# A conv and mixture-of-experts kernel: token tiles in a pool of their own, and the last group's gamma multiply inside the threshold search

## The chip, the cores and the metric

The kernel runs on one core of a Trainium2 chip. The time is that of one execution on the device, in microseconds. Before the change three runs took 4796.59, 4796.63 and 4800.55 us; the median, 4796.63 us, is what a prediction is compared with. One more execution was recorded by the hardware profiler, and every row shown below comes from that one. The engines are called PE (matrix products), DVE (vector), ACT (activation functions), POOL (GpSimd) and SP, which here issues DMAs.

## What is computed

Two layers follow each other. The first is a depthwise 7x7 convolution, a layer norm over channels and a mixture of eight experts with a capacity for each expert; the second is a dilated convolution with an attention in the frequency domain. The change touches only the first, cut here to what matters:

```python
x = depthwise_conv7x7(input) + dw_bias          # 32 x 128 x 56 x 56
xf = layernorm(x) * ln_gamma + ln_beta          # 100352 tokens of 128
topv, topi = top_k(xf @ Wg + bg, 2)             # two of 8 experts
wts = softmax(topv); priority = wts[:, 0]
order = argsort(-priority)                      # tokens by priority
cap = int(1.25 * T / 8)                         # 15680 places an expert
keep = position_in_expert(topi[order]) < cap
y = W2[e] @ gelu(W1[e] @ xf[token] + b1[e]) + b2[e]     # kept pairs
out = input + xf + layer_scale * sum(gate * y)
```

A token keeps its place with an expert if it is among the `cap` tokens of highest priority for that expert. The kernel doesn't sort. For each expert it looks for the threshold of priority by a search over counts, and makes a list of the tokens above it.

## The kernel before

**Conv stage (lines 121 to 391).** Eight groups of images are worked through. A group's tokens are the tile `y` (L376), 98 tokens in each of 128 partitions, 128 channels each, which is 50,176 bytes a partition; there are two such tiles, in the pool `a2`. `conv` fills `y`. Then `block` (L186) does seven pieces of a group (six of 16 tokens, one of 2) in phases: `stats`, `across` (transposes), `norm` (scale and shift by ACT, and by POOL too in the last group), `logits`, `back` and `affine` (L227). `affine` multiplies the normed tokens by gamma (tile `gB`) on DVE at L231 and stores them to the DRAM tensor `xf` at L235. `choose` (L307) takes logits to the two chosen experts (`first1`, `first2`) and their weights (`w1`, `w2`). The phases of a group run beside the conv of the next one. The last group (`end`) has no such neighbour: `plan` (L357) puts its `norm` and `affine` last, `affine` takes up to 8 tokens at a time, at a lower priority, and its stores go out on SP's queue.

**From the last choice to the first list (L507 to L1136).** Pools are laid out as stacks from two sides of the memory. When the conv stage's pools (`a1`, `a2`, `a4`, `a5`) have closed, `b1` and `b2` are opened on the left, and `c1` to `c4`, for the experts, on the right. A pool that is laid where an older one was waits for all of that one's users. After that come, in the order of the source:

- the loads of constants `below`, `lane`, `iota` (into `b1`), of the experts' weights W1 and W2, of `b1t`, `b2t`, `bC` and `lsB` (into `c1`), all on SP's queue, L517 to L529; a small tile `zrow` in `c1`, cleared by DVE at L552;
- `search0` (L677), the search for expert 0. `priorities` (L585) writes `key`; then 12 rounds follow, each with two counts by ACT (`sign`, L702) and one by DVE (`junk`, L706), a sum across partitions by PE (`pn`, L713) and two small DVE steps (`met`, L714, and `lo`, L717). Beside the rounds it does one step each of a list `beside`: eight copies (L671) of transposed choices, made by `turns` (L659), and the keys of expert 0 in their final layout. It ends with `room` (L731);
- `ready` (L558), set-up of tiles for the list, at a lower priority;
- `shift` (L540): 32 products on PE of W1 with the layer norm's beta, L545, added to the experts' bias at L549;
- `listing` (L750) for expert 0: masks, ranks, starts, ten bit steps that move the tokens into place, and the list `ids` (L942). It needs `room` and tiles of `b2`. `search0`, `shift` and `listing` take turns in one single bank of PSUM (`rbank`, L400);
- `fetch` (L1013): gathers of tokens from `xf` by POOL and the experts' matmuls (L1048, L1066).

The order of an engine's instructions is made when the program is built: from the source's order and priorities, and from what the framework takes to be able to run. On the chip each engine takes its queue as it stands.

Of the kernel before, what the change touches and what calls it, by code (L numbers as in the profile page):

```python
# [30 lines left out]
F32 = mybir.dt.float32  # L31
# [7 lines left out]
C = 128  # L39
# [6 lines left out]
E = 8  # L46
# [28 lines left out]
def conv_seq_kernel(ctx: ExitStack, tc: tile.TileContext, t: dict, out: bass.AP, dbg: dict):  # L75
# [43 lines left out]
    w1, w2 = [rk.tile([128, FW], F32, name=f"w{r}") for r in (1, 2)]  # L119

    TG = 2 * NP
    with tc.tile_pool(name="a1", bufs=1) as a1, tc.tile_pool(name="a2", bufs=2) as a2, tc.tile_pool(
# [5 lines left out]
        gB = load(a1, "gB", [128, C], rowbc(t["ln_gamma"], 128))  # L128
# [57 lines left out]
        def block(g, y, lg, t0, n, end):  # L186
# [39 lines left out]

            def affine():  # L227
                with tc.high_priority(offset=-1000) if end else nullcontext():
                    for a in range(0, n, 8 if end else n):
                        cut = slice(a, min(n, a + 8) if end else n)  # L230
                        nc.vector.tensor_tensor(  # L231
                            out=yb[:, cut], in0=yb[:, cut],
                            in1=gB.unsqueeze(1).broadcast_to([128, cut.stop - a, C]), op=ALU.mult,
                        )
                    (nc.sync if end else nc.scalar).dma_start(  # L235
                        out=xfv[:, g * TG + t0 : g * TG + t0 + n, :], in_=yb
                    )
# [137 lines left out]
        for g in range(HI // 2):  # L375
            y = a2.tile([128, TG, C], F32, name="y")  # L376
            for k in range(NS):
                conv(g, k * CB, y)
                if (g, k) == (0, 2):
                    centre()  # L380
                for phase in behind.pop(k, []):
                    phase()
            for k in sorted(behind):
                for phase in behind[k]:
                    phase()
            behind = plan(g, y)
# [122 lines left out]
    b1 = lists_.enter_context(tc.tile_pool(name="b1", bufs=1))  # L509
    b2 = lists_.enter_context(tc.tile_pool(name="b2", bufs=2))  # L510
    experts = ExitStack()
    c1 = experts.enter_context(tc.tile_pool(name="c1", bufs=1, side="right"))
    c2 = experts.enter_context(tc.tile_pool(name="c2", bufs=2, side="right"))
    c3 = experts.enter_context(tc.tile_pool(name="c3", bufs=3, side="right"))
    c4 = experts.enter_context(tc.tile_pool(name="c4", bufs=4, side="right"))
    if True:
        below = load(b1, "below", [128, 128], t["below"])  # L517
# [52 lines left out]
        key = b1.tile([128, E, FW], F32, name="key")  # L570
        share = {}

        apart = set()

        def due(w, f):

            share[f] = w
            return f

        def later(f):  # L580

            apart.add(f)
            return f

        def priorities(e, to=None, cut=slice(0, R), n=FW):  # L585
            to = key[:R, e, :] if to is None else to
            other = b2.tile([128, FW], F32, name="junk", tag="junk")[cut, :n]
            for out_, f in zip((to, other), firsts):
                nc.vector.scalar_tensor_tensor(
                    out=out_, in0=f[cut, :n], scalar=float(E - e), in1=w1[cut, :n], op0=ALU.is_equal, op1=ALU.mult  # L590
                )
            nc.vector.tensor_tensor(out=to, in0=to, in1=other, op=ALU.add)

        thr = b1.tile([128, E], F32, name="thr")
        room = b1.tile([128, E], F32, name="room")

        def search(e0, n):
# [8 lines left out]
            def count(op, at, e):  # L606
                junk = b2.tile([128, FW], F32, name="junk", tag="junk")
                nc.vector.tensor_scalar(
                    out=junk[:R],
                    in0=key[:R, e, :],  # L610
                    scalar1=at[:R],
                    scalar2=None,
                    op0=op,
                    op1=ALU.add,
                    accum_out=part[:, e - e0 : e - e0 + 1],
                )
# [41 lines left out]

        def turns():  # L659

            todo = []
            for a in (w1, *firsts, w2):
                for m0 in range(0, NB, 4):
                    nm = min(4, NB - m0)
                    pt = bank("pkt")
                    for m in range(nm):
                        nc.tensor.transpose(
                            pt[:R, m * 128 : (m + 1) * 128], a[:, bass.DynSlice(m0 + m, R, step=NB)], ident
                        )
                    todo.append(  # L670
                        lambda a=a, pt=pt, m0=m0, nm=nm: nc.vector.tensor_copy(  # L671
                            a[:R, m0 * 128 : (m0 + nm) * 128], pt[:R, : nm * 128]
                        )
                    )
            return todo

        def search0():  # L677


            first = key[:, E - 1, :J]  # L680
            priorities(0, first, slice(0, 128), J)
            k0 = key[:, E - 2, :J]
            beside = turns() + [lambda: priorities(0)]
            lo = b1.tile([128, 1], F32, name="lo")
            nc.vector.tensor_scalar(
                out=k0, in0=first, scalar1=-0.5, scalar2=2.0**24, op0=ALU.add, op1=ALU.mult
            )
            nc.vector.memset(lo, 0.0)
            part = b1.tile([128, 3], F32, name="part0")
            trial = b1.tile([128, 1], F32, name="trial0")  # L690
            less = b1.tile([128, 2], F32, name="less0")
            met = b1.tile([128, 3], F32, name="met0")
            num = b1.tile([128, 1], F32, name="num0")
            for k in range(22, -1, -2):
                q = float(1 << k)
                nc.vector.tensor_scalar(
                    out=less, in0=offs[:, k // 2, :], scalar1=lo, scalar2=None, op0=ALU.subtract
                )
                nc.vector.tensor_scalar(out=trial, in0=lo, scalar1=q, scalar2=None, op0=ALU.add)
                for i in range(2):  # L700
                    sign = b1.tile([128, J], I16, name="sign", tag="sign")
                    nc.scalar.activation(  # L702
                        sign, k0, AF.Sign, bias=less[:, i : i + 1], accum_out=part[:, 1 + i : 2 + i]
                    )
                junk = b2.tile([128, FW], F32, name="junk", tag="junk")
                nc.vector.tensor_scalar(  # L706
                    out=junk[:, :J], in0=k0, scalar1=trial, scalar2=None, op0=ALU.is_ge, op1=ALU.add,
                    accum_out=part[:, 0:1],
                )
                if beside:  # L710
                    beside.pop(0)()
                pn = rbank("pn")
                nc.tensor.matmul(pn[:, :3], lhsT=ones, rhs=part, start=True, stop=True)  # L713
                nc.vector.scalar_tensor_tensor(  # L714
                    out=met, in0=pn[:, :3], scalar=1.0, in1=caps, op0=ALU.mult, op1=ALU.is_ge, accum_out=num
                )
                nc.vector.scalar_tensor_tensor(  # L717
                    out=lo, in0=num, scalar=q, in1=lo, op0=ALU.mult, op1=ALU.add
                )
            nc.vector.tensor_scalar(  # L720
                out=thr[:, 0:1], in0=lo, scalar1=2.0**-24, scalar2=0.5, op0=ALU.mult, op1=ALU.add
            )
            assert not beside
            junk = b2.tile([128, FW], F32, name="junk", tag="junk")
            nc.vector.tensor_scalar(
                out=junk[:, :J], in0=first, scalar1=thr[:, 0:1], scalar2=None, op0=ALU.is_gt, op1=ALU.add,
                accum_out=trial,
            )
            pn = rbank("pn")
            nc.tensor.matmul(pn[:, :1], lhsT=ones, rhs=trial, start=True, stop=True)  # L730
            nc.vector.tensor_scalar(  # L731
                out=room[:, 0:1], in0=pn[:, :1], scalar1=-1.0, scalar2=float(cap + 1), op0=ALU.mult, op1=ALU.add
            )


        caps = b1.tile([128, 3], F32, name="caps")
        nc.gpsimd.memset(caps[:, 0:1], float(cap))
        nc.gpsimd.memset(caps[:, 1:3], float(2 * cap - 128 * J))
        offs = b1.tile([128, 12, 2], F32, name="offs")
        for k in range(12):  # L740
            for i in range(2):
                nc.gpsimd.memset(offs[:, k, i : i + 1], 0.5 - (2 + i) * 4.0**k)
# [7 lines left out]
        def listing(e, ids, gates):  # L750
# [204 lines left out]
            def slots(r, s):  # L955
# [5 lines left out]
                mine = b2.tile([128, FW], F32, name="junk", tag="junk")[:R]  # L961
# [164 lines left out]
        search0()  # L1126
# [548 lines left out]
```

## Time and profile before

| what | us |
|---|---|
| median of three runs | 4796.63 |
| profiled execution (its span) | 5234.6 (5232.8) |
| PE busy in the span | 4638.2 (89%) |
| DVE busy in the span | 2815.0 (54%) |
| one store of 1 MB after another, rate | 283 to 284 GB/s |
| DVE L231 in the last group: first start, last start | 719.6, 740.2 |
| stores `xf<-y` on SP: first, second, last issue | 727.0, 733.8, 747.3 |
| first ACT count of the search | 761.85 |
| PE L545 (`shift`), begin and length | 809.56, 13.8 |
| list `ids` made (DVE L942) | 871.8 |

The profiled execution is 9% longer than the median run; so a stretch of it is compared with other stretches of it, and only then with the runs. The stores before the search, issue by issue: one of 128 KB at 727.0, then six of 1 MB at 733.8, 735.3, 736.8, 739.9, 743.6 and 747.3. How to read a row of the timeline: start, duration, engine, line, operation, the tile written and those read, their shapes, the number of instructions, and in brackets the idle time before it with what ended that. A row of the waits: who waited, on whom, us in total, how often, the longest. Durations of neighbouring DVE rows overlap by about 0.08 us, so the step from one start to the next is shorter than the duration.

### The profile page before, as it was taken

Reading aid. Unit: us, or ns where it says so; the run is one execution under the profiler, and the core shown is the slowest. Engines: PE = TensorE matmul, PEld = TensorE weight load, DVE = VectorE, ACT = ScalarE, POOL = GpSimd, SP = SyncE. Lnnn points to the kernel's source line nnn. Section 1 sums busy time; section 2 is a strip of 40 time slices with the busy share of each in tenths; the row PEclk is TensorE's granted clock in tenths of the full one; section 3 lists DMA queues with packets and bytes.
Section 4 is the critical chain, followed back from the end, with each engine's and each line's share of the span. In section 5 each row is a group of like instructions: output and inputs, shape, how many; then the busy total and the mean of one; then the engine's idle time right before and its main releaser. Section 6 shows DMA issues by size and latency. Waiting matters only on the chain.

```text
span 5232.8 us, 87253 instructions
## 1 busy us (share of the span) xinstructions
PE 4638.2 (89%) x33034; PEld 3216.6 (61%) x33034; DVE 2815.0 (54%) x5851; ACT 2079.8 (40%) x4260; POOL 2610.5 (50%) x2633
## 2 busy tenths in 40 slices
PE   8888844999999999999988799999998888888889
PEld 7777733777777767777766455555555555455556
DVE  4787876868685846442212245555444444444456
ACT  3576742444444444444433133333332222232234
POOL 0000022555555666666466566666566666666650
PEclk9999966999999999999999899999999999999999
DMA  9988940222222323333465455555565565545552
GB/s 254 275 254 261 260 128 17 65 61 66 70 69 71 83 79 87 84 87 87 126 173 135 119 153 161 156 146 151 145 163 150 150 159 155 151 128 151 155 147 57
DMA packets 767736, 705.23 MB, mean 135 GB/s; under 512 B 73231, under 2 KB 679568, under 8 KB 763220
## 3 DMA queue, kind: packets, MB, share of 16 engines
q1 hardware_dynamic: 597060, 487.55, 31.5%
q0 software_dynamic: 81664, 167.15, 14.6%
q10 hardware_dynamic: 88592, 44.96, 3.0%
q8 instruction: 261, 4.28, 0.4%
q14 instruction: 159, 1.30, 0.1%
HBM read 472.99 MB, written 226.39 MB: 134 GB/s over the span
## 4 chain that ended last, share of the span: by engine, by line
PE 74%; DVE 11%; issue 4%; another core or an unknown queue 4%; DMA 3%; ACT 3%; POOL 0%; SPq 0%; DVEq 0%; ACTq 0%; POOLq 0%
PE py L1066 17%; PE ph L1048 16%; PE pf L1283 15%; PE pm L1334 8%; PE pt L1326 4%; DVE st L196 2%; PE pxt L1031 2%; DVE y L231 2%; PE pg L1358 2%; PE pre L1423 2%; DMA xf<-y 2%; ACT y L222 2%; PE pim L1424 2%; PE pxs L1268 2%
## 5 line engine op out<-in xcount | busy, mean ns | idle before, releaser
L444 POOL DMA_INDIRECT y<-yf,slot x1568 | 1547.0, 987 | 972.2 <-issue 352.9
L1025 POOL DMA_INDIRECT xg<-xf,ids x861 | 908.8, 1055 | 710.5 <-PE py L1066 226.8
L1066 PEld LDWEIGHTS py<-W,hT 128*128 128x128 f32 x7872 | 927.2, 192 | 138.9 <-issue 117.1
L1066 PE MATMUL py<-W,hT 128*128 128x128 f32 x7872 | 947.6, 277 | 33.5 <-issue 33.4
L1283 PE MATMUL pf<-xp,cw 128*64 128x448 f32 x4032 | 927.0, 570 | 7.3 <-issue 6.0
L1048 PE MATMUL ph<-xT,W 128*128 128x512 f32 (+1 forms) x1984 | 905.5, 596 | 0.2 <-issue 0.2
L1051 ACT ACTIVATE hT<-ph,b1t 128x512 f32<-128x512 f32 (+1 forms) x992 | 616.7, 672 | 188.2 <-PE ph L1048 129.9
L1313 DVE COPY mid<-pt 112x512 f32<-112x512 f32 (+3 forms) x480 | 310.2, 661 | 572.4 <-PE pt L1326 220.3
L1100 ACT ACTIVATE yo<-yo,gates 128x128 f32<-128x128 f32 x861 | 275.2, 390 | 845.9 <-DVE yo L1080 748.0
L1080 DVE TENSOR_TENSOR yo<-py,b2t 128x512 f32<-128x512 f32 (+2 forms) x256 | 170.5, 669 | 777.7 <-issue 446.5
L1048 PEld LDWEIGHTS ph<-xT,W 128*128 128x128 f32 x1984 | 359.6, 193 | 335.1 <-issue 322.9
L1283 PEld LDWEIGHTS pf<-xp,cw 128*64 128x64 f32 x4032 | 287.3, 140 | 442.2 <-issue 405.6
L217 POOL TENSOR_SCALAR y<-y,sd,nb 128x128 f32<-128x128 f32 x49 | 25.1, 528 | 696.2 <-PE plq L263 695.0
L1337 ACT COPY T<-pm 128x464 f32<-128x464 f32 (+2 forms) x240 | 123.8, 520 | 475.2 <-PE pm L1334 320.2
L222 ACT ACTIVATE y<-y,nb,sd 128x128 f32<-128x128 f32 x735 | 287.5, 481 | 32.3 <-DVE nb L209 32.3
L171 PE MATMUL psa<-xt,stay 112*64 112x98 f32 (+1 forms) x4608 | 233.7, 262 | 43.2 <-DVE y L179 24.2
L1272 DVE SCALAR_TENSOR_TENSOR xp<-pxs,beta,xp 128x256 f32<-128x256 f32 x448 | 173.7, 445 | 153.0 <-PE pxs L1268 48.5
L171 PEld LDWEIGHTS psa<-xt,stay 112*64 112x64 f32 (+1 forms) x4608 | 219.3, 146 | 53.3 <-DVE y L179 29.5
L460 DVE TENSOR_TENSOR xa<-xa,y 128x896 f32<-128x896 f32 x224 | 243.2, 1086 | 2.8
L1291 ACT ACTIVATE feat<-pf,bn_shift,bn_scale 128x448 f32<-128x448 f32 x112 | 81.0, 724 | 398.7 <-remote 133.1
L179 DVE TENSOR_TENSOR y<-psa,dwbB 128x392 f32<-128x392 f32 x256 | 140.2, 556 | 174.7 <-PE psa L171 130.5
L1334 PE MATMUL pm<-ih,mid 116*128 116x112 f32 x928 | 150.0, 309 | 94.8 <-DVE mid L1313 52.6
(412 smaller groups left out, 6204.0 us busy)
## 6 DMA issues: line engine op xcount, KB each, us to landing
xt<-in_x_dram SPq DMA_DIRECT2D x256, 392.0 KB
yf<-yo SPq DMA_DIRECT2D x240, 256.0 KB
xp<-in_xp_dram SPq DMA_DIRECT2D x32, 1832.0 KB
xa<-xf SPq DMA_DIRECT2D x112, 448.0 KB
xsum<-xa SPq DMA_DIRECT2D x112, 448.0 KB
xs<-xsum SPq DMA_DIRECT2D x112, 448.0 KB
xf<-y ACTq DMA_DIRECT2D x42, 1024.0 KB
y<-yf,slot POOLq DMA_INDIRECT x1568
```

The source lines that it names most:

```text
L171: nc.tensor.matmul(ps[h * 64 : (h + 1) * 64, c * TG : (c + 1) * TG], lhsT=wts[b][:, c4 + c, :], rhs=xv[: PKS[b], c, h, :, b * NB : b * NB ...
L222: nc.scalar.activation(yi, yi, AF.Identity, scale=sd[:, i : i + 1], bias=nb[:, i : i + 1])
L444: gated(marks[max(0, n - leash["n"])], nc.gpsimd.indirect_dma_start(out=begun_[r][1][-1][:, m, :], out_offset=None, in_=yf[: 1 + reach(r), :],
L460: nc.vector.tensor_tensor(out=xs, in0=xs, in1=y, op=ALU.add)
L1025: paced(2 * q, nc.gpsimd.indirect_dma_start(out=xg[:n, q, :], out_offset=None, in_=xf, in_offset=bass.IndirectOffsetOnAxis(ap=ids[:n, c0 + ...
L1048: step["pe"] = nc.tensor.matmul(ph[:, :ns], lhsT=W1[:, e, f * C : (f + 1) * C], rhs=xT[:, :ns], start=True, stop=True)
L1051: gelu = nc.scalar.activation(hT[:, f, :ns], ph[:, :ns], AF.Gelu, bias=b1t[:, e, f : f + 1])
L1066: step["pe"] = nc.tensor.matmul(py[:n, q * C : (q + 1) * C], lhsT=hT[:, f, q * 128 : q * 128 + n], rhs=W2[:, e, f, :], start=(f == 0), sto ...
L1100: nc.scalar.activation(yo[:n, q], yo[:n, q], AF.Copy, scale=gates[:n, c0 + q : c0 + q + 1])
L1283: step["pe"] = nc.tensor.matmul(pf[i * DD : (i + 1) * DD, : 8 * W], lhsT=cw[:, k, :], rhs=xps[i][:, o : o + 8 * RP].rearrange("p (h w) -> ...
L1313: step["dve"] = nc.vector.tensor_copy(to, of)
L1334: step["pe"] = nc.tensor.matmul(pm[:, i * M : (i + 1) * M], lhsT=mid[:m, i, :], rhs=by, start=True, stop=True)
```

## The change

The token tiles `y` leave `a2` for a pool `tokens` on the right side, opened before the conv stage's pools and closed after `search0`. `gB` moves from `a1` to `rk`, which lives as long. The last group's `affine` no longer runs in place: it makes pieces of 4 tokens (25 in all) and puts them on a list `scaling`; the piece that completes a block also stores it. `search0` is called before the pools of the lists and experts are opened, on two small pools of its own (`b0`, `bj`); two pieces are called in each of its 12 rounds, what is left behind the rounds. All loads of constants and weights, `zrow` and `ready` come after it in the source, with the code moved as it was.

```diff
+    gB = load(rk, "gB", [128, C], rowbc(t["ln_gamma"], 128))
+    tokens = tc.tile_pool(name="tokens", bufs=2, side="right")
+    ty = tokens.__enter__()
+    scaling = []
...
-        gB = load(a1, "gB", [128, C], rowbc(t["ln_gamma"], 128))
...
+            def scaled(cut):
+                nc.vector.tensor_tensor(
+                    out=yb[:, cut], in0=yb[:, cut],
+                    in1=gB.unsqueeze(1).broadcast_to([128, cut.stop - cut.start, C]), op=ALU.mult,
+                )
+
+            def stored(eng):
+                eng.dma_start(out=xfv[:, g * TG + t0 : g * TG + t0 + n, :], in_=yb)
+
             def affine():
-                with tc.high_priority(offset=-1000) if end else nullcontext():
-                    for a in range(0, n, 8 if end else n):
...
+                if not end:
+                    scaled(slice(0, n))
+                    stored(nc.scalar)
+                    return
+                for a in range(0, n, 4):
+
+                    def piece(a=a):
+                        scaled(slice(a, min(n, a + 4)))
+                        if a + 4 >= n:
+                            stored(nc.sync)
+
+                    scaling.append(piece)
...
-            y = a2.tile([128, TG, C], F32, name="y")
+            y = ty.tile([128, TG, C], F32, name="y")
...
-    b1 = lists_.enter_context(tc.tile_pool(name="b1", bufs=1))
-    b2 = lists_.enter_context(tc.tile_pool(name="b2", bufs=2))
-    experts = ExitStack()
-    c1 = experts.enter_context(tc.tile_pool(name="c1", bufs=1, side="right"))
...
+    b0 = lists_.enter_context(tc.tile_pool(name="b0", bufs=1))
+    bj = lists_.enter_context(tc.tile_pool(name="bj", bufs=2))
     if True:
...
-        key = b1.tile([128, E, FW], F32, name="key")
+        key = b0.tile([128, E, FW], F32, name="key")
...
-                if beside:
-                    beside.pop(0)()
+                for todo in ([beside.pop(0)] if beside else []) + scaling[:2]:
+                    todo()
+                del scaling[:2]
...
             assert not beside
+            while scaling:
+                scaling.pop(0)()
...
+        search0()
+        tokens.__exit__(None, None, None)
+
+        b1 = lists_.enter_context(tc.tile_pool(name="b1", bufs=1))
+        b2 = lists_.enter_context(tc.tile_pool(name="b2", bufs=2))
+        experts = ExitStack()
+        c1 = experts.enter_context(tc.tile_pool(name="c1", bufs=1, side="right"))
...
         scale(0, nc.gpsimd)
-        search0()
         with tc.high_priority(offset=-200):
             ready()
         shift()
```

## The prediction

> **What bounds the kernel at the place of the change.** I read the stages first (the windows view), then the list of waits of 690 to 900 us, then the vector engine's timeline. The conv stage ends at about 700 us, the expert matmuls begin at about 890 us; in between PE is nearly idle and one serial chain runs: last logits, expert choice, the search for expert 0's threshold, its list, the first gathers. From 950 us on PE is 98 to 100% busy, so whatever this chain gains, the end of the kernel should gain.
>
> ```profile
> 745.00:760.00 15.00, 1.68 (x14) 1.48 (x12) 2.36 (x5) 0.00 (x0) 0.94 (x26) 0.61 0.86 236
> 780.00:810.00 30.00, 5.72 (x20) 4.94 (x21) 16.90 (x60) 16.27 (x31) 1.67 (x2) 0.50 0.00 0
> 810.00:830.00 20.00, 14.27 (x68) 14.12 (x68) 6.49 (x10) 0.00 (x0) 0.00 (x0) 0.50 0.00 1
> ...
> 950.00:1000.00 50.00, 49.21 (x290) 36.33 (x289) 41.84 (x90) 22.78 (x50) 28.36 (x25) 1.00 0.24 64
> ```
>
> The numbers after the window's length are busy us of PE, PEld, DVE, ACT, POOL, then clock, DMA share and GB/s. In the first row no engine works and only DMA does: these are the stores of the last tokens. The waits say who stood for them:
>
> ```profile
> POOL caps L737 <- DVE zrow L552: 36.0, 1, 36.0
> POOL W L534 <- DMA lsB<-in_layer_scale_dram: 21.9, 1, 21.9
> DVE zrow L552 <- DMA xf<-y: 15.3, 1, 15.3
> DVE b1t L549 <- PE pb L545: 12.3, 1, 12.3
> ```
>
> `caps` and `zrow` have no data from the stores. They wait because their pools lie where the pools of the conv stage, with `y` in one of them, lay. The vector engine's timeline around that gap:
>
> ```profile
> 719.60 1.22 DVE L231 TENSOR_TENSOR y<-y,gB 128x1024 f32<-128x1024 f32 x1
> ...
> 742.12 0.19 DVE L349 TENSOR_TENSOR w<-top,w 128x34 f32<-128x34 f32 x1
> 757.64 0.17 DVE L552 MEMSET zrow<- 1x128 f32 x1 [15.32 <-DMA xf<-y]
> 757.73 0.90 DVE L589 SCALAR_TENSOR_TENSOR key<-first,w 128x784 f32<-128x784 f32 x1
> ...
> 763.14 0.54 DVE L671 COPY w<-pkt 112x384 f32<-112x384 f32 x1
> 763.61 0.54 DVE L671 COPY first<-pkt 112x384 f32<-112x384 f32 x1
> ```
>
> The last two lines matter as much as the gap. The source gives one such copy to each search round, yet two stand back to back in the first, and all eight are over by 768.2 us, before the third. So an engine's queue is not in source order: work that can run is put into the first hole.
>
> **Part by part.**
>
> *The gap goes.* The search's tiles (`key` 28.7 KB a partition, `junk` twice 3.6 KB, small ones, 38 KB in all by the shapes) fit where a1 lay (41 KB); `y` has moved to its own pool. So `key` waits for the choice alone: 757.73 - 742.31 = **15.4 us gone**.
>
> *Gamma in 25 pieces.* Before, 13 multiplies run between 719.6 and 741.3. One of 1,024 elements costs 1.13 us from start to start, the one of 256 costs 0.33: 12 x 1.13 + 0.33 = 13.9 us inside the choice, which alone would end at 742.3 - 13.9 = 728.4. A piece of 512: between the rows' 407 and 1,210 ns the slope is 1.046 ns an element, so 675 ns, less the 0.08 that neighbours overlap, 0.60 us. Here a rule speaks against the change: the Trainium skill (VectorE: DVE Perf Modes, section "The TRN2 errata") gives an fp32 tensor_tensor (N+151)/0.96 ns, a fixed price per instruction that small tiles pay more often. By it, whole durations added: before 12 x 1.224 + 0.424 = 15.1, after 24 x 0.691 + 0.424 = 17.0, a loss of 1.9 us. The rows have the same durations (1,210 for 1,224; 407 for 424), but in the queue neighbours overlap: 24 x 0.60 + 0.33 = 14.7 against 13.9, a loss of 0.8. I take the row.
>
> *Where the pieces land.* The diff puts two in each round. By the copies above I expect them in the first holes, and the choice has holes: the old multiplies alternated with its steps, 13 of them, and three more gaps follow 741.3 when they had run out. So about 16 pieces stay in the choice (9.6 us), nine go into the search. The choice then ends at 728.4 + 9.6 = 738.0: **4.3 us gained**, bounds 0 (all 25 stay: 728.4 + 14.7 = 743.1, slightly late) and 13.9 (none).
>
> *The search.* From `key` to `room` it takes 757.73 to 809.42, 51.7 us. An undisturbed round is 3.58 us (785.27 to 788.85 from one `met` to the next) with 1.76 us of DVE idle. The first three rounds carried about 8 us of copies and set-up and took 12.9 us for 10.7: fillers cost 0.27 of their length. Nine pieces are 5.4 us: 1.5 us. The transposes that feed the copies, done in the gap before (742.2 to 746.7), now stand beside the search: 0.5. Together **+2 us**, bounds 0 and 6 (nothing hidden).
>
> *A new wait.* Tiles of the experts' pools stand where the tokens stood and wait for the last store. Two first writers are DVE instructions, `zrow` and the cleared edge of `v`, and DVE takes its queue strictly in order (the Trainium skill, PSUM — Partial Sum Buffer, "Engine vs sequencer instructions"; every row here agrees, none tests it), so if they are queued among the rounds before the stores have landed, the search stands still: behind them are its next `met` and `lo`, and ACT and PE wait for those. The trace of before shows such a wait only with nothing else to do (15.3 us). Bounds 0 (it comes later, or falls in a 1.76 us hole) and about 10. Stores: 1 MB goes at 283 GB/s, 3.7 us; four pieces complete a block, so the first store starts at about 724 instead of 733.8, and the last pieces fall at about 750, so the last store lands at about 757. A hole is close by then and the backlog is one or two blocks: I take **+2 us**.
>
> *The experts' loads* are now released by that landing, about 757, as before. From the issue of W1 (759.01) to `lsB` in POOL's hands (780.68) they take 21.7 us, and `bC`, which the PE step L545 needs, is issued just ahead of `lsB`. 757 + 21.7 = 779, before the search's end: hidden, by some 15 us. Without that cover L545 (13.8 us) starts late and all that follows with it. The constants `below`, `lane`, `iota` lie in a pool that still fits beside the tokens and come early. `gB` is loaded one pool earlier, at the start of a 700 us stage: nothing. Gamma of the other groups is as it was: nothing. The POOL memsets (0.9 us) start after the choice's first half instead of at 757.9, and are needed some 3 us after `key` is begun: nothing.
>
> *Behind the search* L545 still starts when `room` is made (809.56 before), the bank of PSUM they share being freed then; the list and the gathers follow unchanged.
>
> **Sum.** Search end: 738.0 + 51.7 + 2 + 2 = 793.7 against 809.4, so **15.7 us earlier**. In the profiled execution 5,232.8 becomes 5,217. That execution (5,234.6 with what lies around its span) is 9% longer than the median of the runs, 4,796.6; the chain is of DVE and ACT steps at fixed durations, so I carry the gain over whole: 4,781 (scaled by 0.917 it would be 14.4, 4,782). I write **4,781.5**.
>
> **Rivals.**
>
> 1. *The pieces are kept to their rounds.* For: that is what the source says. Against: the copies. Then the choice ends at 728.4, the search at 728.4 + 51.7 + 4 = 784, but the last store lands only after it, at about 789; the loads take until 811, L545 until 824.5, against 823.4 before. **No change**, 4,797; with part of the pieces early or DVE standing 6 us or more for stores it is a gain under 9.6 us, and belongs here too.
>
> 2. *The experts' loads become the bound, and it is slower.* The same release, late, with pieces pushed between `met`, `lo` and `trial`, where they hide nothing: each of 25 costs its full 0.60, 15 us. For: set-up steps did stand there (the 0.66 us of `lo` at 781.3 shows how bare this chain is). Against: most of each round's fillers were hidden. Search end 728.4 + 51.7 + 15 = 795, stores 800, loads 822, L545 to 835.6: 12 us late, **4,809**. It decides from the moment the tokens are released later than 809.6 - 21.7 = 787.9.
>
> 3. *More than forecast.* All pieces fall into holes of the search, none into the choice, and the wait is nil: 809.4 - (728.4 + 51.7 + 2) = 27 us, **4,769**. Against: the alternation in the choice.
>
> **How the numbers follow.** Under 0.2% of 4,796.6, 9.6 us, a measurement of this kernel can't be told from no change. Forecast (gain 9.6 to 22) 0.66; rival 3 0.08; rival 1 0.17; rival 2 0.09. Faster 0.74, same 0.17, slower 0.09. The forecast's own range is 4,775 to 4,787. To leave out no more than 2 in 10 I reach to rival 3 and well into rival 1: **4,769 to 4,794**.
>
> **What would show it.** Right: no DVE gap before `key`, which starts at about 738; some 16 rows of L231 with 128x512 between 719 and 738, nine later; the last `xf<-y` issue near 751; L545 directly behind `room`, near 794. Wrong: a DVE wait of more than 5 us for `xf<-y` among the rounds (the in-order wait); L545 waiting for `bC` (rivals 1 and 2); L231 rows still running near the search's end.

## The result, and the profile after

The changed kernel takes 4,781.49 us (median of 6 runs, 4,774.34 to 4,784.02) against 4,797.61 (6 runs, 4,793.73 to 4,800.89). The ratio is 0.996, with a 95% interval of 0.9949 to 0.997: faster by 14 to 24 us, 16 by the medians.

The two profiled executions can't be compared by their spans: 5,232.8 us before, 4,781.7 after. Most of that lies behind 2,500 us, where the change does nothing; the last section comes back to it. I compare the chain instead, and count from one mark that both have, the last logits (`lg<-lg,bgB 128x16`), at 719.52 us before and 717.58 after.

First the list of waits of 690 to 900 us, after:

```profile
POOL W L669 <- DVE trial L593: 46.6, 1, 46.6
DVE b1t L684 <- PE pb L680: 12.3, 1, 12.3
DVE zrow L687 <- DMA xf<-y: 0.3, 1, 0.3
```

The 15.3 us for the stores have become 0.3. `W`, for which POOL stood 21.9 us waiting for `lsB`, now starts at 780.26, while the search still runs, so `lsB` has landed by then at the latest (`trial`, which the line names, is made anew in every round). The wait for L680, which was L545, is unchanged to the tenth: nothing lies beside it still. The windows view, with the prediction's columns:

```profile
745.00:760.00 15.00, 1.76 (x6) 1.50 (x6) 14.08 (x46) 7.13 (x15) 0.00 (x0) 0.50 0.55 149
```

These 15 us, in which the vector engine was busy for 2.36, now hold 14.08 of its work. The vector engine's timeline from the last logits to the first experts' products, with PE's row for these:

```profile
717.58 0.17 DVE L268 TENSOR_TENSOR lg<-lg,bgB 128x16 f32<-128x16 f32 x1
717.66 0.68 DVE L231 TENSOR_TENSOR y<-y,gB 128x512 f32<-128x512 f32 x1
...
735.07 0.19 DVE L363 TENSOR_TENSOR w<-top,w 128x34 f32<-128x34 f32 x1
735.18 0.97 DVE L545 SCALAR_TENSOR_TENSOR key<-first,w 128x784 f32<-128x784 f32 x1
...
747.01 0.15 DVE L609 SCALAR_TENSOR_TENSOR met<-pn,caps 128x3 f32<-128x3 f32 x1
747.09 0.68 DVE L231 TENSOR_TENSOR y<-y,gB 128x512 f32<-128x512 f32 x1
747.69 0.15 DVE L612 SCALAR_TENSOR_TENSOR lo<-num,lo 128x1 f32<-128x1 f32 x1
...
759.51 0.17 DVE L687 MEMSET zrow<- 1x128 f32 x1 [0.28 <-DMA xf<-y]
...
788.67 0.16 DVE L628 TENSOR_SCALAR room<-pn 128x1 f32<-128x1 f32 x1
788.93 13.78 PE L680 MATMUL pb<-bC,W 128*128 128x1 f32 x64 [0.30 <-DVE room L628]
789.34 1.08 DVE L800 TENSOR_TENSOR_SCAN rank<-ones,tie 112x448 f32<-112x448 f32 x1
802.75 0.19 DVE L684 TENSOR_TENSOR b1t<-b1t,pb 128x32 f32<-128x32 f32 x1 [12.33 <-PE pb L680]
802.86 1.08 DVE L800 TENSOR_TENSOR_SCAN rank<-ones,tie 112x448 f32<-112x448 f32 x1
```

`key` stands 0.11 us behind the choice's last row. Of the 25 pieces, 15 start between 717.66 and 734.47, in the choice; one more stands between the first rows of `key`, and nine between 746.4 and 753.4. The rows at 747 show that a piece can stand in a bad place: `met` is made, `lo` is what comes next on the serial chain, and a piece of 0.68 us goes between them. `room` and the products follow each other as before. The last three rows show the in-order wait, though not where the prediction looked for it: a scan in two halves needs only `tie`, which is made by then, yet its second half stands for 12.3 us behind `b1t`, which waits for the products. The kernel before has the same three rows (810.01, 823.41, 823.52); in the run with the products later the two halves follow each other at once (2.06 us for both).

The marks of the chain, in us from the last logits. The step from `room` to expert 0's list of tokens (`ids`) is 62.45 before and 62.48 after:

| kernel | `key` starts | `room` | products start | `ids` made |
|---|---|---|---|---|
| before | 38.21 | 89.82 | 90.04 | 152.27 |
| after | 17.60 | 71.09 | 71.35 | 133.57 |

So the chain gained 18.7 us, 0.39% of 4,797.6, and the measured ratio holds this in its interval.

### The profile page after: what moved, and what is told of

Its sections match the earlier page's. It is cut to its first block, busy times and chain, and to the rows that moved or that the text cites. A ratio compares the mean times of both kernels' runs of the same rounds, so it can differ in the third digit from the quotient of the medians.

```text
span 4781.7 us, 87262 instructions
## 1 busy us (share of the span) xinstructions
PE 4479.7 (94%) x33034; PEld 3134.7 (66%) x33034; DVE 2812.1 (59%) x5863; ACT 2087.5 (44%) x4260; POOL 2627.5 (55%) x2633
## 4 chain that ended last, share of the span: by engine, by line
PE 75%; DVE 3%; DMA 3%; issue 2%; POOL 1%; ACT 0%; DVEq 0%; SPq 0%; POOLq 0%; ACTq 0%
PE py L1089 18%; PE ph L1071 17%; PE pf L1305 16%; PE pm L1356 8%; PE pt L1348 4%; PE pxt L1054 2%; PE pg L1380 2%; DMA y<-yf,slot 2%; PE pre L1445 2%; PE pxs L1290 2%; PE pim L1446 2%; DVE junk L716 1%; POOL y L458 1%; PE pid L956 1%; PE pn L745 1%
## 5 line engine op out<-in xcount | busy, mean ns | idle before, releaser
L458 POOL DMA_INDIRECT y<-yf,slot x1568 | 1567.0, 999 | 559.7 <-issue 318.6
L1089 PE MATMUL py<-W,hT 128*128 128x128 f32 x7872 | 932.5, 276 | 0.0
L1071 PE MATMUL ph<-xT,W 128*128 128x512 f32 (+1 forms) x1984 | 895.3, 590 | 0.0
L1305 PE MATMUL pf<-xp,cw 128*64 128x448 f32 x4032 | 886.7, 549 | 0.1
L1305 PEld LDWEIGHTS pf<-xp,cw 128*64 128x64 f32 x4032 | 276.4, 135 | 410.7 <-issue 373.9
L716 DVE TENSOR_SCALAR_CACHE_REDUCE junk<-key,trial 112x896 f32<-112x896 f32 x168 | 188.7, 1145 | 4.2
```

The lines of the kernel that those rows point to most:

```text
L458: gated(marks[max(0, n - leash["n"])], nc.gpsimd.indirect_dma_start(out=begun_[r][1][-1][:, m, :], out_offset=None, in_=yf[: 1 + reach(r), :],
L1071: step["pe"] = nc.tensor.matmul(ph[:, :ns], lhsT=W1[:, e, f * C : (f + 1) * C], rhs=xT[:, :ns], start=True, stop=True)
L1089: step["pe"] = nc.tensor.matmul(py[:n, q * C : (q + 1) * C], lhsT=hT[:, f, q * 128 : q * 128 + n], rhs=W2[:, e, f, :], start=(f == 0), sto ...
L1305: step["pe"] = nc.tensor.matmul(pf[i * DD : (i + 1) * DD, : 8 * W], lhsT=cw[:, k, :], rhs=xps[i][:, o : o + 8 * RP].rearrange("p (h w) -> ...
```

## The experiments

They ran in two groups of four. On the chip of the first group (layout, kept, more stores, products later) the kernel before took 5,197.9 us, on that of the second (pieces alone, eights, three a round, unaltered) 4,799.8, so each time is given as a ratio to the kernel before in the same group.

**The layout alone.** The changed pools, with the last gamma as it was (13 multiplies, at the old priority):

```diff
-                for a in range(0, n, 4):
-                    def piece(a=a):
...
-                    scaling.append(piece)
+                with tc.high_priority(offset=-1000):
+                    for a in range(0, n, 8):
+                        scaled(slice(a, min(n, a + 8)))
+                    stored(nc.sync)
```

> The new pools and the early search as in the changed kernel, but gamma as before: 13 multiplies, of 8 tokens, at low priority, all inside the choice; no pieces in the rounds. Layout theory (the gain is the 15.4 us gap): all 13 stay ahead of the key, which starts 8.8 + 13.9 = 22.7 us after the first multiply, against 17.5 in the changed kernel and 38.1 before; the search is 1 to 2 us shorter than the changed one's 53.6. Time 4785 (12 us better than before), no DVE wait over 2 us for the stores. Rival, the small pieces are what counts because they bring the last stores forward: here the stores end as late as before, DVE or L545 then waits for them, and less than half of the gain is left: 4790 or more.

Measured: ratio 0.9967 (0.9953 to 0.998). `key` at 22.72, `ids` at 137.34: 14.9 us earlier than before. That is a little more than I wrote, and the rival is out. Most of the gain is the layout; the smaller pieces in the rounds add 3.8 us on the chain.

**The pieces alone.** The kernel before, with one number changed:

```diff
-                    for a in range(0, n, 8 if end else n):
-                        cut = slice(a, min(n, a + 8) if end else n)
+                    for a in range(0, n, 4 if end else n):
+                        cut = slice(a, min(n, a + 4) if end else n)
```

> The kernel before with its last gamma in pieces of 512 instead of 1,024 elements, nothing else: its pools and its priorities stay. My theory, that pieces are worth something only where the search need not wait for the stores: the choice (which ends 22.7 us behind the first multiply in the kernel before) ends some 4 to 5 us earlier, as in the changed kernel (17.5), with about 16 rows of L231 of 128x512 in it and nine behind it; but `zrow` and `key` still wait for the last store, which lands no earlier (38 us behind the first multiply, perhaps 1 later for 25 multiplies instead of 13). Time: no change, between -1 and +5 us against the kernel before, ratio 1.000 to 1.001, `ids` made 152 to 157 us behind the first multiply. The rival, that the finer pieces carry part of the gain by themselves (their blocks are stored earlier, so the wait ends earlier): 3 us or more faster, `key` less than 35.5 us behind the first multiply.

Measured: ratio 1.0008 (1.0002 to 1.0015), 3.8 us slower by the medians. Its vector engine timeline at the end of the choice:

```profile
730.95 0.19 DVE L349 TENSOR_TENSOR w<-top,w 128x34 f32<-128x34 f32 x1
731.05 5.51 DVE L231 TENSOR_TENSOR y<-y,gB 128x512 f32<-128x512 f32 x9
757.42 0.17 DVE L552 MEMSET zrow<- 1x128 f32 x1 [20.87 <-DMA xf<-y]
```

The choice is over sooner, as expected: its last row is 17.6 us behind the mark, and nine pieces are left. The wait for the stores grew from 15.3 to 20.9 us all the same. `ids` come 6.5 us later than before, a little outside what I gave. The DMA view shows why: the steady traffic of the 1 MB stores begins some 21 us behind the mark here, and some 15 in the kernel before (7 in the changed kernel). By then some 20 of the 25 pieces have run here; in the changed kernel the first store is issued 6.3 us behind the mark, after four. That the pieces go around the blocks in turn here, so that the first block is full later, would explain it; no row tells one block's piece from another's, so this is argued and not shown. The same pieces that are worth 3.8 us with the layout cost 6.5 without it.

**Pieces kept to their rounds.** Rival 1 made true: each pair of pieces waits for its round's count.

```diff
-                nc.vector.tensor_scalar(
+                counted = nc.vector.tensor_scalar(
...
-                for todo in ([beside.pop(0)] if beside else []) + scaling[:2]:
-                    todo()
+                if beside:
+                    beside.pop(0)()
+                with tc.issue_after(counted.ins):
+                    for todo in scaling[:2]:
+                        todo()
...
```

> The changed kernel with its 25 pieces held to their rounds: each is queued on DVE behind the count of its own round. Loads theory (what the search gains is worth nothing once the tokens are released late): key about 9 us after the choice's first free step, that is some 9 us earlier than in the changed kernel, room about 780; but the last store lands at about 782, bC 21.7 us later, so L545 waits for it and starts at 803 instead of 788.9. Time 4796, no change from before. Rival, the search alone sets the end: room 8 us earlier and the time with it, 4773.

Measured: ratio 0.9996 (0.9984 to 1.0008). No change, by the way that the rival named (`ids` come 4.5 us earlier than in the kernel before, which this interval also holds). The timeline, first with two rows of the choice:

```profile
718.83 0.69 DVE L333 TENSOR_TENSOR cand<-lg,top 128x512 f32<-128x512 f32 x1
719.56 0.69 DVE L336 TENSOR_TENSOR cand<-cand,revi 128x512 f32<-128x512 f32 x1
...
757.24 1.29 DVE L231 TENSOR_TENSOR y<-y,gB 128x512 f32<-128x512 f32 x2
759.09 0.16 DVE L612 SCALAR_TENSOR_TENSOR met<-pn,caps 128x3 f32<-128x3 f32 x1 [0.56 <-PE pn L611]
...
780.68 0.16 DVE L632 TENSOR_SCALAR room<-pn 128x1 f32<-128x1 f32 x1 [0.68 <-PE pn L631]
783.62 0.37 SPq L96 DMA_DIRECT2D W<-in_W_dram  x1
783.72 0.17 DVE L691 MEMSET zrow<- 1x128 f32 x1 [2.88 <-DMA xf<-y]
...
803.65 1.63 PE L684 MATMUL pb<-bC,W 128*128 128x1 f32 x7 [23.01 <-DMA lsB<-in_layer_scale_dram]
```

`room` is there 7.5 us sooner than in the changed kernel (63.63 from the mark, 71.09 there), since no piece stands in the choice. Then the products wait 23 us: the last store lets go of the tokens at 783.6, and the loads take 20 us from there. Two more things are to be seen. In a round with nothing else beside it, a pair of pieces in the hole behind the count costs nothing: the wait before `met` falls from 1.76 to 0.56, and the round stays at 3.59 (759.09 from 755.50). And the 2.9 us of `zrow` are no test of the in-order wait: it stands behind `room`, and `tie`, next in the queue, lies in `b2`, which is laid in part where the tokens were and so, by the rule of the pools, waits for the last store itself.

**More stores.** Each of the last stores is followed by two more of the same data to a place that nobody reads, so that the tokens are held three times as long. This adds work and takes none away.

```diff
...
                 eng.dma_start(out=xfv[:, g * TG + t0 : g * TG + t0 + n, :], in_=yb)
+                if end:
+                    for c in range(2):
+                        nc.sync.dma_start(out=xtv[:, c * TG + t0 : c * TG + t0 + n, :], in_=yb)
```

> The changed kernel with each of the last group's seven stores followed by two more of the same size to a tensor that nobody reads (added work, output as it was). 19 MB at 283 GB/s take 68 us from about 724, so the last lands at about 792. Loads theory: bC at 792 + 21.7 = 814, L545 starts there instead of at 788.9, everything after is 25 us later: 4806, slower than before; room itself stays at about 789, since the first DVE writer of the experts' pools is queued behind room here. Rival, the stores are hidden whenever they end (only the DVE order counts): 4782.

Measured: ratio 1.0006 (0.9994 to 1.0018), so the whole gain is gone; that it is slower than the kernel before, as I wrote, is not shown. `room` is at 69.90, even earlier than in the changed kernel; the products start at 98.09, and `ids` come at 159.26, 25.7 us later than there. The cover of the loads is gone, and everything behind it moves: rival 2's mechanism exists. By the prediction it decides from a release 68.4 us behind the mark (787.9 there); W1 is issued at 76.1 here, and at 41.8 in the changed kernel. SP is busy with the stores and small loads in front until 75.5, so this run does not separate the held tokens from the queue; the one kept to its rounds does, since SP is done with its stores at 780.1 there and W1 still waits until 783.6.

**The pieces larger.** The changed kernel with pieces of 8 tokens (1,024 elements) in its rounds, in place of 4.

```diff
-                for a in range(0, n, 4):
+                for a in range(0, n, 8):
...
-                        scaled(slice(a, min(n, a + 4)))
-                        if a + 4 >= n:
+                        scaled(slice(a, min(n, a + 8)))
+                        if a + 8 >= n:
```

> The changed kernel with pieces of 1,024 elements instead of 512, as thirteen of them, still in rounds and still free to move. My theory: the same number of holes in the choice takes all twelve large ones, so the choice ends 9.6 - 13.6 = about 4 to 5 us later than in the changed kernel (`key` 22 to 23 us behind the first multiply instead of 17.5), the search has 5.4 us of fillers less and is shorter by 1.5 to 4 us, and `zrow`, now queued in an early round, can hold the vector engine for 3 to 6 us until the last store has landed. Together 3 to 8 us slower than the changed kernel: `ids` 137 to 141 us behind the first multiply, where the changed kernel has 133.5; against the kernel before -7 to -14 us. The rival, that the size of the piece does not matter: `ids` at 133.5 and 18 us better than before.

Measured: ratio 0.9969 (0.9959 to 0.9979), which the clock can't tell from the unaltered kernel beside it (0.9972). On the chain my theory is half right. All thirteen stand in the choice (`key` at 22.60, five later), and the search from `key` to `room` is shorter by 2.2 us, 51.25 against 53.49. But `zrow` waits for nothing, since the pieces end sooner (W1 is issued 29.3 us behind the mark, and 41.8 in the changed kernel), so the loss is 2.75 us (`ids` at 136.32) and not 3 to 8.

**The products later.** With `room` early, the row directly behind it is next: 13.8 us of PE for which DVE waits 12.3. What they make, `b1t`, is needed only by the first expert. Here they are issued from the list's ninth step, and the addition to `b1t` behind the first of the values:

```diff
...
-        shift()
...
-        for s in steps:
+        for i, s in enumerate(steps):
             s()
+            if i == 8:
+                pb = shift()
+            if i == len(steps) - 3:
+                with tc.issue_after(made["vl"].ins):
+                    shifted(pb)
```

> The changed kernel with the 32 products L545 moved in the source from before the list to behind its starts, so that PE does them under the ten bit steps of DVE, and the addition L549 queued behind the last bit step. If L545 is on the path (12.3 us of DVE wait at L549 in both profiles): the list is made 12 to 12.5 us earlier, time 4769. Rival, it was only in front of another wait (the gathers, W1): less than 4 us, 4778 or more.

Measured: ratio 0.9944 (0.9921 to 0.9966). The timeline:

```profile
800.02 1.15 DVE L888 SCALAR_TENSOR_TENSOR v<-rank,start,keep 112x896 int16<-112x896 f32 x1
800.11 4.22 PE L680 MATMUL pb<-bC,W 128*128 128x1 f32 x19 [2.76 <-DVE start L864]
801.09 0.15 DVE L865 TENSOR_SCALAR start<-start 112x1 f32<-112x1 f32 x1
...
833.40 0.18 DVE L687 TENSOR_TENSOR b1t<-b1t,pb 128x32 f32<-128x32 f32 x1
833.52 1.22 DVE L944 SCALAR_TENSOR_TENSOR val<-v,val 112x1024 f32<-112x1024 int16 x1
```

DVE goes on beside the products, and `b1t` costs it 0.12 us with no wait. `ids` are 121.06 behind the mark, 12.5 us before the changed kernel's. The changed kernel was not measured on this chip; its own ratios, 0.996 and 0.9972, have intervals that reach into this one, so that the products' gain rests on the chain.

**Three pieces a round, with the products later.** What the runs before pointed to: if no load is on the path, the pieces belong into the holes of the rounds. The edit is that of the pieces kept to their rounds with `scaling[:3]`, and that of the products later with step 13 in place of 8.

> The run with the shift's products moved, with the pieces in another way: three in each of the first rounds, none allowed ahead of its round's count, so none in the choice; the products five list steps later. My theory: where no load is on the path any more, the pieces belong into the 1.76 us hole of each round, which two of them (1.29 us) left at 3.58 us; three take 1.8 us and fill it. The choice ends 7 us earlier (10.3 us behind the logits instead of 17), the search loses 1 to 2 us by the pieces, the last store lands at about 768 us and `bC` at about 790, before the products are due at about 803. `ids` 5 to 7 us earlier than in the run with the products moved, 830 to 834 us there 838.7; time 17 to 20 us better than the changed kernel and 35 us better than the kernel before, ratio 0.993. The rival: the last store holds the vector engine at `zrow` as in the run with the pieces kept (2.9 us) or longer, and the loads hold the products: no better than the run with the products moved, 29 us and ratio 0.9944.

Measured: 4,764.47 us against 4,799.75, ratio 0.9932 (0.9918 to 0.9946), the best of all, and clear of the unaltered kernel's on the same chip (0.9961 to 0.9983, below). The timeline of two rounds, and of the wait that the rival named:

```profile
755.36 1.89 DVE L231 TENSOR_TENSOR y<-y,gB 128x512 f32<-128x512 f32 x3
757.21 0.16 DVE L612 SCALAR_TENSOR_TENSOR met<-pn,caps 128x3 f32<-128x3 f32 x1
...
758.95 1.89 DVE L231 TENSOR_TENSOR y<-y,gB 128x512 f32<-128x512 f32 x3
760.79 0.16 DVE L612 SCALAR_TENSOR_TENSOR met<-pn,caps 128x3 f32<-128x3 f32 x1
...
766.74 0.17 DVE L692 MEMSET zrow<- 1x128 f32 x1
```

Three pieces are 1.89 us in a hole of 1.76, and the round is still 3.58. Not every round is so empty: where a copy or a key stands in the hole too, the pieces do lengthen it. `zrow` has no bracket: it waits for nothing. `ids` are at 115.90, 5.2 us before the run with the products moved.

**The changed kernel once more.**

> The changed kernel once more, unaltered, on the chip of the experiments, to have its gain beside theirs. If the 16 us of the first measurement are those of the chain (18.7 us earlier `ids` in the trace, less 1 to 3 us that come back behind them): 16 to 19 us better than the kernel before, ratio 0.9963 to 0.997. If the gain scaled with the chip's time (5,198 against 4,798 us), 17 us, which this measurement does not tell from it.

Measured: ratio 0.9972 (0.9961 to 0.9983), 14.2 us by the medians, a little less than I wrote, with my ratios inside the interval. The chain is the same within 0.01 us: `key` 17.61, `room` 71.10, `ids` 133.57.

All together, in us from the last logits, with the chain's change in `ids` as a ratio to the kernel before's time in the same group:

| kernel | `key` | `room` | products | `ids` | by `ids` | measured |
|---|---|---|---|---|---|---|
| layout alone | 22.72 | 74.88 | 75.13 | 137.34 | 0.9971 | 0.9967 (0.9953 to 0.998) |
| pieces alone | 44.14 | 96.34 | 96.55 | 158.80 | 1.0014 | 1.0008 (1.0002 to 1.0015) |
| kept to rounds | 10.44 | 63.63 | 86.60 | 147.79 | 0.9991 | 0.9996 (0.9984 to 1.0008) |
| more stores | 17.68 | 69.90 | 98.09 | 159.26 | 1.0013 | 1.0006 (0.9994 to 1.0018) |
| pieces larger | 22.60 | 73.85 | 74.11 | 136.32 | 0.9967 | 0.9969 (0.9959 to 0.9979) |
| products later | 17.61 | 71.09 | 82.50 | 121.06 | 0.9940 | 0.9944 (0.9921 to 0.9966) |
| three a round, products later | 10.44 | 64.97 | 77.32 | 115.90 | 0.9924 | 0.9932 (0.9918 to 0.9946) |
| unaltered | 17.61 | 71.10 | 71.36 | 133.57 | 0.9961 | 0.9972 (0.9961 to 0.9983) |

Every measured interval holds what the chain says, the last at its very edge. What `ids` gain or lose, the end of the kernel gains or loses, as far as these runs can tell. But in seven of the eight the measured ratio is nearer to 1 than the chain's, so a part of it, some microseconds, may come back behind `ids`; that stays open.

## Why the prediction was right

It was right in the time (4,781.5 written) and in the mechanism, which the rows it had named bear out. That the median fell on the number is luck: on the chain the gain was 18.7 us for 15.7, errors of single steps partly cancelled, and the same kernel measured again gained 14.2. Its steps, in us from the last logits:

| step | predicted | measured |
|---|---|---|
| the choice without any piece | 8.9 | 10.4 (kept to rounds) |
| pieces in the choice | 16, at 0.60 | 15, at 0.48 |
| `key` starts | 18.5 | 17.6 |
| search, with its fillers | 51.7 + 2 | 53.2 |
| in-order wait at `zrow` | 2 (0 to 10) | 0.3 |
| `room` | 74.2 | 71.1 |
| `lsB` reaches POOL | 59.5 | 62.7 |
| `ids` earlier by | 15.7 | 18.7 |

*The gap* is gone as stated, and the run with the layout alone puts its share at 14.9 of the 18.7 us.

*The pieces in the choice.* The count of holes was right but for one. The price was off twice, in opposite directions. The two runs without pieces there show the choice alone at 10.44. So 15 pieces add 17.60 - 10.44 = 7.2 us, 0.48 each and not 0.60: the choice has short stalls of its own, which a piece fills in part. With pieces kept to rounds the dependent rows L333 and L336 are 0.73 us apart (718.83 to 719.56); in the changed kernel, with a piece between them, 1.20 (720.50 to 721.70), so that piece costs 0.47. Taking the old multiplies off at their full step of 1.13 made the choice alone too short, for the same reason.

*Row against rule.* The Trainium skill's rule (VectorE: DVE Perf Modes, section "The TRN2 errata") and the row that I took instead both made the finer cut a loss, of 1.9 and of 0.8 us. Both priced how long the multiplies occupy the engine. By the run with larger pieces the finer cut gains 2.75 us on the chain, since fewer elements are left in the choice: 15 pieces of 512 stand there in place of twelve of 1,024 and the small one. The durations were right; what decides is which of them lie in front of `key`.

*The search.* Two microseconds for the fillers were about right (53.2 for 51.7, and 53.5 with the wait). Where a filler stands decides its price: behind the count of a round with nothing else in its hole, none; between `met` and the count, about half. Over the whole search, which takes 52.16 us with the layout alone and no pieces, all 25 cost about 1.0 us with two a round (53.19) and 2.4 with three (54.53). From one `met` to the next the changed kernel's round with five pieces is 751.47 - 747.01 = 4.46 us for 3.58: two of the five stand in the hole, and the other three cost 0.88 of their 1.80.

*The in-order wait* is the term that was over-estimated: 0.28 us for the 2 taken, because `zrow` came up just as the last store landed, which is luck too. That DVE keeps its order is shown by the second half of the scan, 12.3 us behind `b1t`. The prediction said that no row tests this; the kernel before has that row, and the prediction passed it over.

*The loads* were hidden, by less than the 15 us given: `lsB` is in POOL's hands at 780.26 and `room` starts at 788.67, 8.4 us. They came 3 us later than predicted, since the last pieces and with them the last store did (issued at 753.5, 35.9 us behind the mark, where the prediction's 751 is 31.5), and the search ended 3 us sooner. The run with more stores shows what the cover is worth.

*Rival 1* was priced well: no change, `room` 64.5 from the mark (784), and 63.6 in the run made so; the products' end 105.0 (824.5), and 100.4, where the kernel before has 103.9. It did not come about because the pieces do move into the first holes, as the copies before had. *Rival 2* needs a release that even the pieces kept to rounds did not quite reach (66.6 from the mark against 68.4); with the stores added it came. *Rival 3* had no loads in its sum: with no piece in the choice `room` does come 26.2 us earlier than before (63.63 for 89.82, where it had 27), but the tokens are then let go so late that the products wait 23 us.

*Two readings of the profile before.* That no engine works in the window of 745 to 760 us holds from 746.8 to 757.6; DVE's 2.36 us lie behind that. And PE is not 98 to 100% busy all the way from 950 us on: behind 2,500 the window in the last section has 889.29 of 1,000. That the end gains what the chain gains rests on the measured ratios above, not on this.

## What to carry to other kernels

Free work has no price of its own: the same multiply cost 0 in an otherwise empty hole behind the count, 0.48 of its 0.60 us in a busy serial stage, and about half between two small dependent steps, so cost it by the place in which the scheduler will put it. Parts of a change don't add up: the finer pieces were worth 3.8 us where nothing waited for their stores, and cost 6.5 where something did. When a wait goes, look at the row that then stands at the end of the chain; here it was 13.8 us of products that only the first expert needs, and moving them and the pieces together gave twice the gain of the change on the chain (36.4 us for 18.7).

## What the runs showed of the hardware

The kernel before took 4,798 us in one group of runs, 4,800 in another and 5,198 in the third, and the profiled execution of before, 5,232.8 us, is like the last. The chain knows nothing of that: from `room` to `ids` the kernels that kept that stretch take 62.45 to 62.48 us on all of them. Most of the difference lies in the long stretch of matmuls behind 2,500 us. Windows of before and of after, same columns as above:

```profile
2500.00:3500.00 1000.00, 889.29 (x5055) 571.62 (x5056) 364.45 (x613) 336.90 (x645) 597.09 (x608) 0.94 0.55 146
```

```profile
2500.00:3500.00 1000.00, 982.61 (x6030) 633.29 (x6028) 463.34 (x789) 382.61 (x708) 706.38 (x712) 0.99 0.66 177
```

At a clock of 0.94 for 0.99 the same window holds 5,055 matmuls for 6,030, far fewer than the ratio of the clocks, with PE busy for less of it. The typical matmul is as long in both: over the whole executions the median of the products `pf<-xp,cw` is 537 ns, before (L1283) and after (L1305). So PE stands idle for longer, and the clock alone does not explain the slower execution. A part may be that it has other work in this window; the cause is not settled here.

The second thing is SP's queue under a backlog. In the run with more stores, SP's issues:

```profile
726.62 0.40 SPq L239 DMA_DIRECT2D xf<-y  x1
727.08 5.55 SPq L253 DMA_DIRECT2D xtwice<-y  x2
732.79 3.50 SPq L239 DMA_DIRECT2D xf<-y  x1
...
794.28 0.42 SPq L96 DMA_DIRECT2D below<-in_below_dram  x1
```

The first issue takes 0.40 us. Once transfers are outstanding, one of 1 MB holds SP for about 3.5, as long as its data takes (3.7 us by the prediction's rate). So `below`, which waits for no token and is issued at 735.46 in the changed kernel, stands in line behind the stores until 794.28.
